# The last ranking of a four-layer expert kernel: row adds moved forward, final sums moved to another engine, 16-bit ranks, and matrix products that nobody reads

## The chip, the cores and the metric

The kernel runs on one core of a Trainium2 chip. A core has a matrix engine (PE, with its weight loads shown apart as PEld), a vector engine (DVE), a scalar or activation engine (ACT), a general engine (POOL, GpSimd) and SP, which here only issues transfers. Each engine takes its instructions in order; the engines run side by side and wait for one another on semaphores. Tiles live in on-chip memory with 128 partitions; PE writes its sums into PSUM.

The metric is the time of one execution on the device in microseconds (us). Before the change three runs took 1600.47, 1604.69 and 1605.46 us; the median is 1604.69.

## The reference

2048 tokens of 256 channels pass through four layers; each adds `ffn(cond(x))` to `x`. The change touches only the feed-forward part of the last layer, in which each of 16 experts takes at most 160 tokens, those with the highest gate value:

```python
cap = math.ceil(1.25 * bt / n)               # bt = 2048 tokens, n = 16 experts: 160
probs = softmax(x @ Wg)                      # (2048, 16)
top1_val, top1_idx = probs.max(-1), probs.argmax(-1)
masked = where(top1_idx[None, :] == arange(n)[:, None], top1_val[None, :], -inf)
vals, idx = top_k(masked, cap)               # per expert: its 160 best tokens
valid = isfinite(vals)
h = gelu(einsum('ncd,ndh->nch', x_flat[idx], W1) + b1[:, None, :])
out = einsum('nch,nhd->ncd', h, W2) + b2[:, None, :]
y_flat = x_flat.at[where(valid, idx, bt)].set(out, mode='drop')
# the layer before hands in x_flat; the kernel's result is x + y_flat
```

A token that no expert keeps passes `x_flat` itself on. So the result of every token is first `x + x_flat`, and the rows of the kept tokens are written again with `x + out`.

## The kernel before, in words

The 2048 tokens are 16 tiles of 128 (index t) and four blocks of 512 (index q). `Xt` holds the residual `x` by rows of tokens, `Ht` (in the memory `ACC`) the layer's input `x_flat` by rows, `HT` the same by channels.

**How `Ht` is finished.** The conditioning part of layer 3 (`_cond_moe`) ends with a shared expert, computed block by block in `_shared`: products `spg`, `spu`, a gate `sa` on DVE (L1232), products `spo` (L1235). Meanwhile the class `Tokens` adds the routed experts' rows: for each token tile SP loads two rows per token (`yt`), DVE adds them times a gate to `Ht` (L1321, two instructions a tile), and PE transposes the tile into `HT`. The list `by` says how many tiles have been added by each step of the last shared block; what is left is done by `pair`, two tiles a call, in `finish`.

**The last ranking** (class `Last`, four `chunk`s, one for each block q). A chunk is a list of small units:

- `logits`: writes the block to the DRAM tensor `hx` (its right half, written earlier, holds `Xt`), and multiplies it by the gate weights (`l3f_pt`).
- `top`: transposes the logits (`l3f_pl`); DVE finds the chosen expert and the softmax value.
- `rows`: DVE makes the one-hot of the expert (`l3f_oh`) and a bf16 row `l3f_z` of one-hot and the value split into three bf16 parts (with the small subtractions `l3f_r`, L1812); PE turns it (`l3f_ps`, L1816), and counts earlier tokens of the expert (`l3f_pn`).
- 4q+4 `beats`: one for each token tile t up to the block. A product `l3f_d` compares 128 tokens with 512; DVE (even t, L1855) or ACT (odd t, L1852) turns the signs into `l3f_b` and counts along the rows, and a second product adds them by columns (`l3f_cs`). After the last beat of a block `l3f_pc` brings the column counts into `l3f_acc`.

After `rows` of each block, `keep` adds `Ht` to `Xt` on GpSimd (L1876, 128x1024) and SP writes the block to the kernel's output (512 KB, L1877). Block 0's units and the first one of others are called by `plan` inside the steps of the shared expert; the rest in the order of the list `todo`, in `finish`, which a scheduler then spreads over the engines.

**From ranks to experts.** `l3f_acc` summed is twice each token's rank within its expert. DVE compares the rank with 0..159 (`l3f_A`, two halves of 128x1280, L1914), 32 products `l3f_pi` (L1919) turn that into the token of each rank, and DVE makes indices of them (`numbers`; `l3f_src`, and after a small product `l3f_pj` `l3f_srcg` for ranks 128 to 159 of four experts at a time). GpSimd gathers 128 rows of `hx` for each expert (L338) into one of six slots in `ACC`; PE transposes them (`ps_cm`, L360), multiplies (`l3f_ph`, `l3f_po`), and GpSimd scatters the result to the output. There are 16 such steps and four for the groups of four experts. The bias rows `b2` (for single experts) and `b2g` (for the groups) are loaded by SP, `b2g` into the memory of `Ht` once it is read.

Of the kernel before, what the change touches and what calls it, by code (L numbers as in the profile page):

```python
# [8 lines left out]
F32 = mybir.dt.float32  # L9
# [77 lines left out]
def _consts(k):  # L87
    nc, cp = k.nc, k.cp
    k.ident = cp.tile([P, P], F32, name="ident")
    make_identity(nc, k.ident)  # L90
    k.ones = cp.tile([P, P], F32, name="ones")
    nc.vector.memset(k.ones, 1.0)

    k.before = cp.tile([P, P], F32, name="before")
    nc.gpsimd.affine_select(out=k.before, in_=k.ones, compare_op=ALU.is_ge, fill=0.0,
                            base=-1, pattern=[[1, P]], channel_multiplier=-1)

    k.ident16 = cp.tile([P, P], BF16, name="ident16")
# [12 lines left out]
    nc.vector.tensor_copy(k.iota, ii)  # L111
    nc.vector.memset(k.zero[:, 0:D], 0.0)
    nc.vector.memset(k.zero[:, D:], NONE)
    it = cp.tile([P, NT], I32, name="it")
    nc.gpsimd.iota(it, pattern=[[P, NT]], base=0, channel_multiplier=1)
    k.tok = cp.tile([P, NT], F32, name="tok")
    nc.vector.tensor_copy(k.tok, it)
    k.tok2 = cp.tile([P, NT], F32, name="tok2")
    nc.vector.tensor_scalar_mul(k.tok2, k.tok, 2.0)
    k.one16 = cp.tile([P, P], BF16, name="one16")  # L120
    nc.vector.memset(k.one16, 1.0)
    k.two = cp.tile([P, 1], F32, name="two")
# [230 lines left out]
    return ps.rearrange("p c d -> p (c d)")  # L353


def _channel_major(k, psum, rows):

    ps = psum.tile([P, 2, P], F32, name="ps_cm", tag="t", bufs=2)
    for c in range(2):
        k.nc.tensor.transpose(ps[:, c, :], rows[:, c * P:(c + 1) * P], k.ident)  # L360
    return ps


# [845 lines left out]
                                             mybir.DependencyReason.SCHED_ONLY))  # L1209


def _shared(k, pool, psum, X, tb, W1, W3, W2, nf, hook=None, mid=None):


# [82 lines left out]
class Tokens:  # L1297
# [4 lines left out]
    def __init__(self, k, pool, psum, gate, dst, dstT, nf, next=None):  # L1302
        self.k, self.pool, self.psum, self.gate = k, pool, psum, gate
        self.dst, self.dstT, self.next = dst, dstT, next
        self.h = self.added = self.put = self.there = 0
        self.done = None
        self.mul = None

        self.by = [0, 0, 1, 3, 4, 6, 7, 9, 10, 12, 13, 15, 16, 16, 16, 16] if nf == 8 else \
                  [0, 0, 1, 3, 4, 6, 8, 10]  # L1310

    def add(self, t, ref=None):
        k, d = self.k, self.dst[:, t, :]
# [370 lines left out]
class Last:  # L1684
# [73 lines left out]
    def chunk(self, q):  # L1758
# [75 lines left out]
        def beats(t):  # L1834

            def unit(mul, mm):
# [27 lines left out]
                if t == 4 * q + 3:  # L1864
# [1 line left out]
                    nc.scalar.activation(less, got["cs"][0:1, :], AF.Copy, scale=-1.0)  # L1866
                    ps = psum.tile([P, 4], F32, name="l3f_pc", tag="t", bufs=2)
                    for j in range(4):
                        nc.tensor.matmul(ps[:, j:j + 1], less[:, j * P:(j + 1) * P], k.ones[0:1, 0:1],  # L1869
                                         start=True, stop=True, skip_group_check=True)  # L1870
                    nc.vector.tensor_copy(self.acc[:, ts, 6], ps)
            return unit

        def keep(mul, mm):
            x = k.Xt[:, ts, :]
            nc.gpsimd.tensor_tensor(x, x, k.Ht[:, ts, :], ALU.add)  # L1876
# [3 lines left out]
        def last(mul, mm):  # L1880
            rows(mul, mm)
            keep(mul, mm)

        return [logits, top, last] + [beats(t) for t in range(4 * q + 4)]

    def finish(self, c):

# [2 lines left out]
        for e in range(E):  # L1890
            nc.sync.dma_start(self.b2[:, e, :], k.A["L3_b2"][e:e + 1].to_broadcast([P, D]))
        self.weights()
        p0, p1, p2, p3 = self.parts
        todo = [c.pair, p0[0:2], p1[0:1], c.pair, p1[1:2], p0[2:4], c.pair, p2[0:1], p0[4:], p1[2:3], p2[1:2],
                p1[3:7], p3[0:1], p1[7:], p2[2:3], p3[1:2], p2[3:7], p3[2:3], p2[7:], p3[3:]]
        for x in todo:
            if callable(x):
                x()
            else:
                for p in x:  # L1900
                    p(None, None)
        assert c.put == NT
        self.b2g = k.Ht[:, 12:16, :]
# [4 lines left out]
        rank = k.rp.tile([P, NT], F32, name="l3f_rank")  # L1908
        nc.vector.tensor_reduce(rank, self.acc, AX.X, ALU.add)
        nc.vector.tensor_scalar_mul(rank, rank, 0.5)  # L1910
        ps = k.psum.tile([P, 2, 2, E], F32, name="l3f_pi", tag="t", bufs=2)
        for h in range(2):
            A = k.pool.tile([P, 8, CAP], BF16, name="l3f_A", tag="fa")
            nc.vector.tensor_tensor(A, _bc(k.iota, 1, [P, 8, CAP]),  # L1914
                                    _bc(rank[:, 8 * h:8 * h + 8], 2, [P, 8, CAP]), ALU.is_equal)
            for j in range(8):
                t = 8 * h + j
                for o, r in ((ps[:, 0], slice(0, P)), (ps[0:32, 1], slice(P, CAP))):
                    nc.tensor.matmul(o, A[:, j, r], self.ids[:, t], start=t == 0 and r.start == 0,  # L1919
                                     stop=t == NT - 1, skip_group_check=True)  # L1920
        self.src, self.dst = self.numbers(ps[:, 0], E, "")

        more = k.rp.tile([32, 2, E], F32, name="l3f_more")
        nc.vector.tensor_copy(more, ps[0:32, 1])
        pg = k.psum.tile([P, 2, 4], F32, name="l3f_pj", tag="t", bufs=2)
        for g in range(4):
            nc.tensor.matmul(pg[32 * g:32 * g + 32], k.ident[0:32, 0:32], more[:, :, g::4], start=True,
                             stop=True, skip_group_check=True)
        s, d = self.numbers(pg, 4, "g")
        self.src, self.dst = ([t[:, i:i + 1] for t, n in ((a, E), (b, 4)) for i in range(n)]  # L1930
                              for a, b in ((self.src, s), (self.dst, d)))

    def numbers(self, ps, n, name):

# [14 lines left out]
    def run(self):  # L1949
        k, nc, E, F = self.k, self.k.nc, self.E, self.F  # L1950
        pool, psum, b1 = k.pool, k.psum, k.small["L3_b1"]
        X = k.ACC.rearrange("p c s -> p (c s)").rearrange("p (b f) -> p b f", f=2 * D)

        order = [x for i in range(4) for x in (*range(4 * i, 4 * i + 4), E + i)]
        order = order[:-3] + [order[-1]] + order[-3:-1]
# [2 lines left out]
        def fetch(n):  # L1958
            if n < len(order):
                i = order[n]  # L1960
                at[i] = X[:, n % 6, :]
                _gather(k, at[i], k.hx, self.src[i])

        def end(i, po, b2):
# [54 lines left out]
            fetch(n)  # L2019
        for n, i in enumerate(order):  # L2020
            xT = pool.tile([P, 2, P], F32, name="xsT", bufs=3)
            nc.vector.tensor_copy(xT, _channel_major(k, psum, at[i]))
            if i < E:
                end(i, slot(i, xT), self.b2[:, i, :])
            else:
# [151 lines left out]
```

## Time and profile before

| what | value |
|---|---|
| median of three runs | 1604.69 us (1600.47 to 1605.46) |
| the profiled execution, and its span | 1597.45 us, 1595.3 us |
| mean granted clock of PE over the span | 0.964 |
| last shared block, to its last `spo` | until about 1434 us of the span |
| ranking: first `l3f_ps` | 1440.69 us |
| ranking: last copy of `l3f_pc` | 1483.99 us |
| one-hots `l3f_A` | 1484.80 us, 2.89 us for two |
| first gather issued, first transpose of gathered rows | 1492.58 us, 1496.12 us |
| experts at full clock | from about 1503.7 us |

The trace gives for each instruction its start and length, and what ended the idle time before it; `[2.70 <-DVE l3f_z L1810]` reads: the engine was idle for 2.70 us, until DVE's instruction of line 1810 was done. A group "x8" is eight instructions of one line in a row, with their busy time in sum. The windows give, for a stretch of the span, the busy time of each engine with its number of instructions, then the granted clock of PE (1.00 is full speed), the share of the transfer engines and GB/s. The chain of waits is the path back from the last instruction to what released each step.

### The profile page before, as it was taken

How to read it: one execution, taken by the hardware profiler on the slowest of the kernel's cores; microseconds unless marked ns; L12 is line 12 of the kernel's file. 1: busy time of each engine (PE TensorE's matmuls, PEld its weight loads, DVE VectorE, ACT ScalarE, POOL GpSimd, SP SyncE). 2: the span in 40 equal slices, each digit the busy share in tenths (PEclk: the TensorE clock that was granted, in tenths of full speed). 3: DMA queues.
4: the chain of work that ended last, by engine and by line, in shares of the span. 5: the costliest groups of instructions: out<-in, count | busy, mean ns of one | idle time of the engine just before them, and what ended most of it. 6: DMA issues, size and time to landing. Idle time of an engine off the chain costs nothing. (4 is left out here: it accounts for less than half of the span.)

```text
span 1595.3 us, 23657 instructions
## 1 busy us (share of the span) xinstructions
PE 1478.0 (93%) x8583; PEld 1024.6 (64%) x8586; DVE 475.0 (30%) x1586; ACT 303.3 (19%) x641; POOL 294.0 (18%) x321
## 2 busy tenths in 40 slices
PE   6979998967999989999999999999999999997797
PEld 2543333533555876555599999999995558864575
DVE  3732221323411344341111111111114414446332
ACT  2312221112111212111111111111112212125222
POOL 0400000200231332023100000000000163421242
PEclk9889999977999999999999999999999999998799
DMA  9769994813211465051152444255507357674171
GB/s 253 256 206 334 349 345 151 241 55 119 83 50 40 143 216 181 27 192 53 34 179 75 132 166 146 74 179 182 178 11 267 103 173 242 192 221 138 62 242 36
DMA packets 184242, 252.47 MB, mean 158 GB/s; under 512 B 17111, under 2 KB 137823, under 8 KB 184112
## 3 DMA queue, kind: packets, MB, share of 16 engines
q1 hardware_dynamic: 164448, 210.92, 40.7%
q0 software_dynamic: 14176, 36.63, 6.5%
q10 hardware_dynamic: 5488, 3.25, 0.7%
q8 instruction: 74, 1.21, 0.3%
q14 instruction: 56, 0.46, 0.1%
HBM read 284.86 MB, written 50.76 MB: 210 GB/s over the span
## 5 line engine op out<-in xcount | busy, mean ns | idle before, releaser
L283 POOL DMA_INDIRECT tbuf<-ys,sdst x114 | 112.2, 984 | 537.3 <-ACT ys L1438 228.4
L1235 PE MATMUL spo<-ring,sa 128*128 128x256 f32 x768 | 191.7, 392 | 14.0 <-DVE sa L1232 14.0
L1235 PEld LDWEIGHTS spo<-ring,sa 128*128 128x128 f32 x768 | 140.1, 191 | 95.9 <-DVE sa L1232 76.0
L1232 DVE TENSOR_TENSOR sa<-ssg,spu 128x512 f32<-128x512 f32 x96 | 65.9, 687 | 325.3 <-PE spu L1225 302.8
L1429 PE MATMUL fpg<-xsT,ring 128*128 128x128 f32 x1152 | 141.6, 276 | 5.9 <-ACT ys L1438 5.9
L1429 PEld LDWEIGHTS fpg<-xsT,ring 128*128 128x128 f32 x1152 | 135.8, 192 | 10.4 <-ACT ys L1438 9.4
L1429 PE MATMUL fpu<-xsT,ring 128*128 128x128 f32 x1152 | 140.4, 275 | 0.0
L1429 PEld LDWEIGHTS fpu<-xsT,ring 128*128 128x128 f32 x1152 | 134.4, 192 | 0.0
L1433 DVE TENSOR_TENSOR fa<-fsg,fpu 128x512 f32<-128x512 f32 x72 | 49.5, 688 | 276.9 <-PE fpu L1429 276.9
L1436 PE MATMUL fpo<-ring,fa 128*128 128x256 f32 x576 | 130.3, 379 | 0.0
L1230 ACT ACTIVATE ssg<-spg 128x512 f32<-128x512 f32 x96 | 57.3, 597 | 341.2 <-PE spg L1225 333.2
L1436 PEld LDWEIGHTS fpo<-ring,fa 128*128 128x128 f32 x576 | 106.7, 190 | 13.0
L1225 PE MATMUL spg<-HT,ring 128*128 128x512 f32 x192 | 101.2, 615 | 5.1 <-PEq L484 2.9
L1225 PE MATMUL spg<-XT,ring 128*128 128x512 f32 x192 | 99.0, 605 | 4.7 <-ACT XT L902 4.7
L1412 PE MATMUL cpo<-ring,ch 128*128 128x256 f32 x312 | 87.0, 402 | 5.8 <-ACT ch L1409 4.1
L1225 PE MATMUL spu<-HT,ring 128*128 128x512 f32 x192 | 91.1, 595 | 0.0
L1225 PE MATMUL spu<-XT,ring 128*128 128x512 f32 x192 | 90.5, 594 | 0.0
L1406 PEld LDWEIGHTS cph<-xsT,ring 128*128 128x128 f32 x624 | 81.8, 191 | 5.0 <-ACT ch L1409 1.1
L1406 PE MATMUL cph<-xsT,ring 128*128 128x128 f32 x624 | 82.4, 275 | 0.7 <-ACT ch L1409 0.7
L1379 DVE COPY xsT<-ps_cm 128x256 f32<-128x256 f32 x138 | 56.7, 422 | 82.5 <-PE ps_cm L360 81.9
L1432 ACT ACTIVATE fsg<-fpg 128x512 f32<-128x512 f32 x72 | 43.0, 597 | 179.6 <-PE fpg L1429 179.6
L1412 PEld LDWEIGHTS cpo<-ring,ch 128*128 128x128 f32 x312 | 53.1, 189 | 21.2 <-ACT ch L1409 15.1
(567 smaller groups left out, 1599.1 us busy)
## 6 DMA issues: line engine op xcount, KB each, us to landing
ring<-in_L_w SPq DMA_DIRECT2D x108, 1024.0 KB
ring<-in_L_r SPq DMA_DIRECT2D x96, 512.0 KB
ring<-in_L_r SPq DMA_DIRECT2D x156, 256.0 KB
xs<-xbuf SPq DMA_DIRECT2D x138, 129.0 KB
ring<-in_L_W SPq DMA_DIRECT2D x32, 512.0 KB
yt<-tbuf SPq DMA_DIRECT2D x48, 256.0 KB
xbuf<-ACC SPq DMA_DIRECT2D x1, 6063.0 KB
ring<-in_L_s SPq DMA_DIRECT2D x6, 512.0 KB
```

Of the source, the lines that this page charges most:

```text
L283: i = k.nc.gpsimd.indirect_dma_start(out=self.ap, out_offset=bass.IndirectOffsetOnAxis(ap=idx, axis=0), in_=rows, in_offset=None, **end)
L1225: mm = nc.tensor.matmul(ps, W[:, c, f * P:(f + 1) * P], X[:, c, cols], start=c == 0, stop=c == 1)
L1230: nc.scalar.activation(sg, pg, AF.Silu)
L1232: mul = nc.vector.tensor_mul(a, sg, pu)
L1235: mm = nc.tensor.matmul(po[g // 2][:, g % 2, :], a[:, g * P:(g + 1) * P], W2[:, f, :], start=f == 0 and g % 2 == 0, stop=f == nf - 1, skip ...
L1379: turned = nc.vector.tensor_copy(xT, _channel_major(k, self.psum, xs))
L1406: nc.tensor.matmul(ph[:, f, :], R1[:, c, f * P:(f + 1) * P], xT[:, c, :], start=c == 0, stop=c == 1)
L1412: nc.tensor.matmul(po, h[:, f, :], R2[:, f, :], start=f == 0, stop=f == 1)
L1429: nc.tensor.matmul(ps[:, j, :], W[:, c, (f0 + j) * P:(f0 + j + 1) * P], xT[:, c, :], start=c == 0, stop=c == 1)
L1432: nc.scalar.activation(sg, pg, AF.Silu)
L1433: nc.vector.tensor_mul(a[:, f0:f0 + 4, :], sg, pu)
L1436: nc.tensor.matmul(po, a[:, f, :], W2[:, f, :], start=f == 0, stop=f == 4 * nh - 1)
```

## The change

- `by` adds the row tiles earlier (12 instead of 10 within the shared steps), and `plan` has block 1's logits at the last of them.
- `todo` is reordered: both pairs of tiles first, then tops and rows of all blocks ahead of their beats; the 28 beats of blocks 2 and 3 come last, together.
- `keep` is gone. The four sums `Xt += Ht` are made by DVE behind the second `l3f_A`; the four writes of the output follow them, and the loads of `b2g` follow the writes.
- The ranks are compared in bf16, with a bf16 copy of the numbers 0..159.
- `_warm` adds six 128x512 bf16 products behind the last `l3f_pc`, ahead of `l3f_pi`, and ten behind `l3f_pj`, ahead of the first `ps_cm`. Nothing reads their results.
- The gathers go to `HT`, which has eight slots, instead of `ACC` with six.

As the scheduler places it, DVE's order at the end is: both `l3f_A`, the sum of block 0, the copy of `l3f_pi`, the sum of block 1, four more small steps, the sum of block 2, the cast `l3f_src`, three steps and the cast `l3f_dst`, the sum of block 3, the rest. Line numbers in the kernel after are those of before plus 2 from L112 on and plus 4 to 17 in the functions below.

```diff
+    k.iota16 = cp.tile([P, CAP], BF16, name="iota16")
+    nc.vector.tensor_copy(k.iota16, ii)
...
+def _warm(k, psum, ref, n):
+    ps = psum.tile([P, TB], F32, name="warm", tag="mm")
+    for _ in range(n):
+        i = k.nc.tensor.matmul(ps.rearrange("p (j q) -> p j q", q=P), k.ident16, _bc(k.ident16, 1, [P, 4, P]),
+                               start=True, stop=True, skip_group_check=True)
+        _behind(k, i, ref)
+        ref = i
+    return ref
...
-                  [0, 0, 1, 3, 4, 6, 8, 10]
+                  [0, 0, 2, 4, 6, 8, 10, 12]
...
-        self.plan = {5: [0], 6: [0], 7: [0]}
+        self.plan = {5: [0], 6: [0], 7: [0, 1]}
...
-        def keep(mul, mm):
-            x = k.Xt[:, ts, :]
-            nc.gpsimd.tensor_tensor(x, x, k.Ht[:, ts, :], ALU.add)
-            i = nc.sync.dma_start(k.out[cols, :].rearrange("(t p) d -> p t d", p=P), x)
-            self.outs.append(i.ins.name)
...
-        todo = [c.pair, p0[0:2], p1[0:1], c.pair, p1[1:2], p0[2:4], c.pair, p2[0:1], p0[4:], p1[2:3], p2[1:2],
-                p1[3:7], p3[0:1], p1[7:], p2[2:3], p3[1:2], p2[3:7], p3[2:3], p2[7:], p3[3:]]
+        todo = [c.pair, c.pair, p1[0:1], p2[0:1], p3[0:1], p0, p2[1:2], p1[1:2], p3[1:2], p1[2:], p2[2:3],
+                p3[2:3], p2[3:], p3[3:]]
...
+        ref = _warm(k, k.psum, ref, 6)
...
+        rank16 = k.rp.tile([P, NT], BF16, name="l3f_rank16")
+        nc.vector.tensor_scalar_mul(rank16, rank, 0.5)
...
-            nc.vector.tensor_tensor(A, _bc(k.iota, 1, [P, 8, CAP]),
-                                    _bc(rank[:, 8 * h:8 * h + 8], 2, [P, 8, CAP]), ALU.is_equal)
+            made = nc.vector.tensor_tensor(A, _bc(k.iota16, 1, [P, 8, CAP]),
+                                           _bc(rank16[:, 8 * h:8 * h + 8], 2, [P, 8, CAP]), ALU.is_equal)
...
+        self.ref = _warm(k, k.psum, ref, 10)
...
+        for q in range(NB):
+            x = k.Xt[:, 4 * q:4 * q + 4, :]
+            _behind(k, nc.vector.tensor_tensor(x, x, k.Ht[:, 4 * q:4 * q + 4, :], ALU.add), made)
+            i = nc.sync.dma_start(k.out[q * TB:(q + 1) * TB, :].rearrange("(t p) d -> p t d", p=P), x)
+            self.outs.append(i.ins.name)
         self.b2g = k.Ht[:, 12:16, :]
...
-        X = k.ACC.rearrange("p c s -> p (c s)").rearrange("p (b f) -> p b f", f=2 * D)
+        X = k.HT.rearrange("p c n -> p (c n)").rearrange("p (b f) -> p b f", f=2 * D)
...
-                at[i] = X[:, n % 6, :]
+                at[i] = X[:, (n + 4) % 8, :]
```

`_behind` orders one instruction after another on its engine. `_channel_major` makes `ps_cm`, and its transposes now stand behind the ten products.

More of the change, by code (lines that the diff above doesn't have):

```diff
@@ L353, in _token_major, with _channel_major @@
     return ps.rearrange("p c d -> p (c d)")
-def _channel_major(k, psum, rows):
+def _channel_major(k, psum, rows, ref=None):
     ps = psum.tile([P, 2, P], F32, name="ps_cm", tag="t", bufs=2)
     for c in range(2):
-        k.nc.tensor.transpose(ps[:, c, :], rows[:, c * P:(c + 1) * P], k.ident)
+        i = k.nc.tensor.transpose(ps[:, c, :], rows[:, c * P:(c + 1) * P], k.ident)
+        if ref is not None:
+            _behind(k, i, ref)
     return ps
@@ L1209, in _behind @@
                                              mybir.DependencyReason.SCHED_ONLY))
+def _warm(k, psum, ref, n):
[3 more added lines that the diff above has]
+                               start=True, stop=True, skip_group_check=True)
+        _behind(k, i, ref)
+        ref = i
+    return ref
 def _shared(k, pool, psum, X, tb, W1, W3, W2, nf, hook=None, mid=None):
@@ L1868, in unit @@
                     for j in range(4):
-                        nc.tensor.matmul(ps[:, j:j + 1], less[:, j * P:(j + 1) * P], k.ones[0:1, 0:1],
+                        i = nc.tensor.matmul(ps[:, j:j + 1], less[:, j * P:(j + 1) * P], k.ones[0:1, 0:1],
                                          start=True, stop=True, skip_group_check=True)
                     nc.vector.tensor_copy(self.acc[:, ts, 6], ps)
+                    return i
             return unit
-        def keep(mul, mm):
-            x = k.Xt[:, ts, :]
-            nc.gpsimd.tensor_tensor(x, x, k.Ht[:, ts, :], ALU.add)
-            i = nc.sync.dma_start(k.out[cols, :].rearrange("(t p) d -> p t d", p=P), x)
-            self.outs.append(i.ins.name)
[L1880 to L1884, printed above, removed]
+        return [logits, top, rows] + [beats(t) for t in range(4 * q + 4)]
     def finish(self, c):
@@ L1893, in finish @@
         p0, p1, p2, p3 = self.parts
-        todo = [c.pair, p0[0:2], p1[0:1], c.pair, p1[1:2], p0[2:4], c.pair, p2[0:1], p0[4:], p1[2:3], p2[1:2],
-                p1[3:7], p3[0:1], p1[7:], p2[2:3], p3[1:2], p2[3:7], p3[2:3], p2[7:], p3[3:]]
+        todo = [c.pair, c.pair, p1[0:1], p2[0:1], p3[0:1], p0, p2[1:2], p1[1:2], p3[1:2], p1[2:], p2[2:3],
+                p3[2:3], p2[3:], p3[3:]]
+        ref = None
         for x in todo:
@@ L1900, in finish @@
                 for p in x:
-                    p(None, None)
+                    ref = p(None, None) or ref
+        ref = _warm(k, k.psum, ref, 6)
         assert c.put == NT
+        rank = k.rp.tile([P, NT], F32, name="l3f_rank")
+        nc.vector.tensor_reduce(rank, self.acc, AX.X, ALU.add)
+        rank16 = k.rp.tile([P, NT], BF16, name="l3f_rank16")
+        nc.vector.tensor_scalar_mul(rank16, rank, 0.5)
+        ps = k.psum.tile([P, 2, 2, E], F32, name="l3f_pi", tag="t", bufs=2)
+        for h in range(2):
+            A = k.pool.tile([P, 8, CAP], BF16, name="l3f_A", tag="fa")
+            made = nc.vector.tensor_tensor(A, _bc(k.iota16, 1, [P, 8, CAP]),
+                                           _bc(rank16[:, 8 * h:8 * h + 8], 2, [P, 8, CAP]), ALU.is_equal)
+            for j in range(8):
+                t = 8 * h + j
+                for o, r in ((ps[:, 0], slice(0, P)), (ps[0:32, 1], slice(P, CAP))):
+                    i = nc.tensor.matmul(o, A[:, j, r], self.ids[:, t], start=t == 0 and r.start == 0,
+                                         stop=t == NT - 1, skip_group_check=True)
+                    _behind(k, i, ref)
+        self.src, self.dst = self.numbers(ps[:, 0], E, "")
+        more = k.rp.tile([32, 2, E], F32, name="l3f_more")
+        nc.vector.tensor_copy(more, ps[0:32, 1])
+        pg = k.psum.tile([P, 2, 4], F32, name="l3f_pj", tag="t", bufs=2)
+        for g in range(4):
+            ref = nc.tensor.matmul(pg[32 * g:32 * g + 32], k.ident[0:32, 0:32], more[:, :, g::4], start=True,
+                                   stop=True, skip_group_check=True)
+        self.ref = _warm(k, k.psum, ref, 10)
+        s, d = self.numbers(pg, 4, "g")
+        self.src, self.dst = ([t[:, i:i + 1] for t, n in ((a, E), (b, 4)) for i in range(n)]
+                              for a, b in ((self.src, s), (self.dst, d)))
+        for q in range(NB):
[3 more added lines that the diff above has]
+            self.outs.append(i.ins.name)
         self.b2g = k.Ht[:, 12:16, :]
@@ L1907, in finish @@
                               k.A["L3_b2"][e:e + 1].to_broadcast([32, D]))
[L1908 to L1914, printed above, removed]
-                                    _bc(rank[:, 8 * h:8 * h + 8], 2, [P, 8, CAP]), ALU.is_equal)
[L1916 to L1931, printed above, removed]
     def numbers(self, ps, n, name):
@@ L2021, in run @@
             xT = pool.tile([P, 2, P], F32, name="xsT", bufs=3)
-            nc.vector.tensor_copy(xT, _channel_major(k, psum, at[i]))
+            nc.vector.tensor_copy(xT, _channel_major(k, psum, at[i], self.ref))
             if i < E:
```

## The prediction

> **What bounds the kernel now.** I read the page first, for the whole, then the windows of the stage that changes (1422 to 1505 us of the span), then its timeline on each engine, and last the chain of waits. The page:
>
> ```profile
> span 1595.3 us, 23657 instructions
> ...
> PE 1478.0 (93%) x8583; PEld 1024.6 (64%) x8586; DVE 475.0 (30%) x1586; ACT 303.3 (19%) x641; POOL 294.0 (18%) x321
> ...
> PEclk9889999977999999999999999999999999998799
> ```
>
> TensorE is the bound of the span, but the share says nothing of 83 us in the last tenth, where the granted clock dips (digits 8, 7). The windows there (columns: PE, PEld, DVE, ACT, POOL, granted clock, DMA share):
>
> ```profile
> 1440.00:1452.00 12.00, 9.41 (x76) 5.98 (x76) 7.13 (x31) 4.91 (x15) 0.54 (x1) 0.73 0.66 236
> 1452.00:1462.00 10.00, 6.79 (x46) 3.97 (x47) 7.13 (x33) 3.97 (x11) 1.96 (x1) 0.64 0.43 144
> ...
> 1472.00:1484.00 12.00, 10.88 (x62) 5.78 (x61) 6.21 (x22) 8.63 (x23) 0.00 (x0) 1.00 0.01 2
> 1484.00:1492.00 8.00, 4.82 (x40) 3.51 (x40) 4.46 (x14) 0.15 (x1) 0.00 (x0) 0.65 0.00 0
> ...
> 1496.00:1500.00 4.00, 3.19 (x14) 2.85 (x15) 0.42 (x1) 0.00 (x0) 2.93 (x4) 0.50 0.66 205
> ```
>
> PE has holes in 1440–1462 and, after its last beat, in 1484–1500; in both the clock falls to about half. Finer windows put the half-clock stretches at 1442.5–1445.5, 1449–1459.1 and 1486.5–1503.7. The timeline says who makes the holes:
>
> ```profile
> 1451.46 2.49 POOL L1876 TENSOR_TENSOR Xt<-Xt,ACC 128x1024 f32<-128x1024 f32 x1 [13.12 <-DVE ACC L1321]
> ...
> 1451.64 2.33 DVE L1812 TENSOR_TENSOR l3f_r<-l3f_val,l3f_z 128x4 f32<-128x4 f32 x1
> ...
> 1454.80 1.03 PE L1816 MATMUL l3f_ps<-ident,l3f_z 128*128 128x128 bf16 x8 [2.70 <-DVE l3f_z L1810]
> ...
> 1462.59 0.61 PE L1816 MATMUL l3f_ps<-ident,l3f_z 128*128 128x128 bf16 x8
> ...
> 1468.76 0.62 PE L1816 MATMUL l3f_ps<-ident,l3f_z 128*128 128x128 bf16 x8 [0.72 <-DVE l3f_z L1810]
> ...
> 1483.99 0.17 DVE L1871 COPY l3f_acc<-l3f_pc 128x4 f32<-128x4 f32 x1 [2.51 <-PE l3f_pc L1869]
> ...
> 1484.80 2.89 DVE L1914 TENSOR_TENSOR l3f_A<-iota,l3f_rank 128x1280 bf16<-128x1280 f32 x2
> ...
> 1486.35 4.53 PE L1919 MATMUL l3f_pi<-l3f_ids,l3f_A 128*128 128x32 bf16 x32 [2.40 <-DVE l3f_A L1914]
> ...
> 1491.54 0.17 DVE L1942 CAST l3f_src<-l3f_i 128x16 uint32<-128x16 f32 x1
> ...
> 1492.58 1.00 POOL L338 DMA_INDIRECT ACC<-hx,l3f_src  x1 [38.63 <-DVE l3f_i2g L1943]
> ...
> 1496.12 0.66 PE L360 MATMUL ps_cm<-ident,ACC 128*128 128x128 f32 x2 [4.30 <-DMA ACC<-hx,l3f_src]
> ```
>
> A four-column subtraction that takes 0.16 us elsewhere takes 2.33 us beside GpSimd's add, and PE's rows of block 1 (`ps` at 1454.80) wait for it. From 1484 on nothing overlaps: rank, one-hots, `pi`, indices, gather, first expert. The chain of waits runs the same way:
>
> ```profile
> 1451.72 2.25 DVE l3f_r L1812
> ...
> 1454.80 1.03 PE l3f_ps L1816 x8
> ...
> 1486.35 4.54 PE l3f_pi L1919 x32
> ...
> 1493.89 3.45 DMA ACC<-hx,l3f_src
> ...
> 1497.92 3.41 PE l3f_ph L1980 x16
> ```
>
> **The change, part by part** (us; before is always the profiled execution).
>
> *Row adds earlier, logits of block 1 at step 7.* Two pairs of token rows instead of three remain after the last shared step. Steps there wait on row loads: DVE waited 4.29, 0.36 and 2.75 on `yt` (1418.07, 1420.43, 1431.24), and PE's `spo` waited 0.91, 0.41 and 0.95 on DVE's `sa` behind them. One more add now stands before the second `sa`, whose rows land about 1419.4 by the issue pitch of 0.85; that `spo` comes 1.1 to 1.5 later, and the later two waits shrink, because SP no longer issues the first `out` write (1425.16) ahead of their loads. Net +0.9 at the last `spo`, bounds 0 and +1.5. The rows of block 3 still load behind `b2` and a weight on SP (1430.63 to 1436.26): 0 to +2, inside the bounds below. The writes of `hx`, of blocks 2 and 3, move ahead of `out`; the last was issued 41 before the first gather: 0, and it would cost only if that cover shrank below the 3.45 a gather takes.
>
> *Final sums off GpSimd.* Its four adds (2.36, 2.35, 2.35, 2.49) go. Two held DVE up: 2.42 at 1436.01 where 0.22 is usual, and 2.33 at 1451.64. The first gives back 2.2, which covers the late start: `ps` of block 0 comes at 1440.3 instead of 1440.7. The second, and logits made earlier, bring `ps` of block 1 from 1454.80 to 1450.3 (bounds 1449.3, all of 5.4 gained, and 1451.3).
>
> *The new order.* Block 1 to block 2: eight beats at 0.527 (the last 24 beats took 12.6, 1469.66 to 1482.3) = 4.2, `pn` 0.85, `pc` 1.05, the transpose and its pause 0.9: 7.0, so 1457.3. Block 2 to the end of block 3's `pn` took 7.27 with four beats between; without them 7.27 - 2.1 = 5.2, and 0.6 less where the `z` wait of 0.72 runs beside `pn`: 4.6, so 1461.9. Then 28 beats, 14.75, to 1476.65; from the last beat to the copy of `pc` 1.7 (1482.3 to 1483.99): 1478.4. That is **-5.6** against 1483.99. The bounds: 0, if the beats in one run wait for `b` slots and PE's clock as much as the mixed order did; -9, if none of PE's holes stays (they sum to 10.8 in 1435–1484, less what rows must still wait). I take -5.6, nearest to the rows of 1469–1484, which are already such a run of beats and at full clock.
>
> *Ranks compared in bfloat16.* The two one-hots took 2.89, 1.45 each. Bounds: 0, and half of it, -0.75 for the first and -1.45 in all. I take 0. The trace has no 16-bit compare of a broadcast operand; casts of `z` to bf16 show nothing faster than their f32 neighbours (0.23 beside 0.22). [...] The extra copy of iota at the start is one 128x160 copy, under 0.3 in a DVE idle for 70%: 0, or +0.3 without that cover.
>
> *Products nobody reads, before `pi`.* Six 512-column bf16 products, 0.215 each at full clock, 1.3 in all, stand in PE's wait of 2.40 for the first one-hot. Alone they cost 0 (+1.3 if the wait were gone). If PE keeps the full clock, `pi` and `pj` end about 1.9 sooner after the second one-hot (32 products that spread over 1487.7–1490.9 at half clock). Bounds 0 and -1.9.
>
> *Sums on DVE behind the one-hots.* Four adds of 128x1024. Rows: 128x512 f32 at 0.687, 128x1280 at 1.45; between them 1.14 each. DVE is in order, and two of them end up inside the chain of indices (after the first index steps and ahead of the cast of `src`): +2.3 (one, +1.1; none, if they fit the wait of 3.22 for `pi`, 0). With the gain of `pi`, copy of `pc` to cast of `src` is 7.74 instead of 7.55: **+0.2**, +2.1 if the clock falls first.
>
> *Writes of `out` late.* Four writes of 512 KB, on SP, no longer beside the ranking but beside the first gathers; the 16 loads of `b2g` queue behind them (first used at the fifth gather's expert group, far later). At the 380 to 390 GB/s seen in 1441–1446 a write takes 1.4. The first gather took 3.45; behind one or two writes it takes +0.5 to +2.8. I take **+1.0**, since two of the four sums come after the index cast. Scatters wait for these writes too, but start some 15 later. Gathers into HT (eight slots for six) let GpSimd issue eight ahead of the first scatter instead of six: one each 1.25, nobody waits for the sixth: 0 to -0.3.
>
> *Products before the first transpose.* Ten, 2.2 at full clock; PE waits 4.30 for the gather. If they held the clock, `ph` and `po` would not start at half rate to 1503.7: -3.0 (six of half-clock stretch, 1497.7–1503.7). The trace's clock edges at 1442.45, 1445.5, 1448.96, 1459.1, 1486.5 and 1503.7 lie on one grid of about 3.41. [...] By the grid of the trace alone the bounds are the same, 0 and -3.0; I take half, **-1.6**.
>
> Sum: -5.6 + 0.2 + 1.0 - 1.6 = **-6.0**. The experts from 1505 to 1586 are PE at clock 1.00 with the same products, and the last scatters follow them: unchanged. On the profiled execution, 1597.45 - 6.0 = 1591.4 (its span 1595.3 and 2.15 around it). That execution lies 7.2 below the median of the three runs, 1604.69, so the median becomes 1598.7; I give **1598**, a shade lower, as more of the bounds lie below -6.0 than above.
>
> **The rivals.** (a) *Slower: the clock stays low in the ranking.* At half clock a bf16 product takes 0.43 (`cs`, 1458.60) and a beat has two: 0.86 instead of 0.527. If the tops and rows of blocks 1 to 3, now gathered at 1441–1462, leave PE short of work long enough that the clock is still half during the 36 beats behind them, they cost 36 x 0.333 = +12; less 5.6, and with the tail's +0.2 + 1.0 and no clock gain there: +7.6, 1612. From 28 beats at half clock on it passes +4.8. For it: windows of 0.73 and 0.64 at a PE duty of 0.68 to 0.78. Against: 28 beats in one run are at 0.91 duty and 1.00. (b) *The tail takes it back:* three sums in the index chain (+3.4), two writes ahead of the gather (+2.8), no clock gained: +5 to +6, against -5.6: 0 for the whole, about 1604. For it: DVE in order, and a DMA queue that was empty (0.01, 0.00) and no longer is. Against: the first sums fit PE's time in `pi`. (c) *More:* -9 in the ranking, clock kept to the experts (-3), the gather undisturbed: -11 to -12, 1593. (d) *The parts do nothing:* beats stay bound at 0.527 with the old holes moved, 16-bit compare and products without effect: -1 to -2, 1603.
>
> **How the numbers follow.** Chances: forecast (-4 to -9) 0.50, (c) 0.17, (b) 0.11, (d) 0.09, (a) 0.13. What a measurement can tell from no change is 0.3%, 4.8. Faster by more: 0.46 of the forecast, all of (c), 0.04 of (b) and (d) in milder forms: 0.67. Same: 0.04 of the forecast, 0.12 of (b) and (d), 0.02 of a mild (a): 0.18. Slower: 0.11 of (a), and 0.04 for (b) with nothing gained in the ranking: 0.15. The range reaches from (c) counted from the lowest run, 1600.47 - 11 = 1589.5, to (b) at the highest, 1605.46, so 1606; it leaves out (a) and a few of (c). For the forecast alone, 1595.7 to 1600.7.
>
> **What would show it.** Right: no 2.3 stall on `r` and no POOL add; `ps` of block 1 near 1450; the copy of `pc` near 1478; the one-hots still 1.45 each; two sums of about 1.1 to 1.2 between the index steps; the first gather's landing 3.5 to 5 after issue; the experts' clock back within 3 of `ps_cm`. Wrong: granted clock under 0.8 in windows of the last beats; beats slower than 0.55; DVE still in a sum when PE has finished `pj` for 2 us; a first `ps_cm` that waits over 6. I would be most wrong if the clock in the ranking, which I read from windows, is set by something other than PE's own holes.

## The result and the profile after

The kernel after took 1603.66 us (median of 20 runs, 1598.26 to 1608.57), the kernel before 1603.61 us (20 runs). The ratio is 0.9996, 95% interval 0.9984 to 1.0009: no difference that can be told. (The ratio is that of the means of the 20 runs; the medians are as good as equal.) The forecast of 1598 us is missed by 5.7 us. The time lies in the range, which holds no change at all as well, at the place where rival (b) had put it; the prediction gave "faster" 0.67 and "same" 0.18.

The profiled execution of after took 1608.57 us, with a span of 1606.7 us, 11 us longer than the one of before. Those 11 us lie ahead of the changed stage: the first `spo` of the last shared block starts at 1425.32 us instead of 1414.36 (in the experiments below, between 1411.82 and 1423.55). So the two traces are compared by stages counted from that `spo`, in us:

| stage | before | after | difference | forecast |
|---|---|---|---|---|
| first `spo` to last copy of `l3f_pc` | 69.63 | 66.07 | -3.56 | -5.6 |
| copy of `l3f_pc` to cast of `l3f_src` | 7.55 | 9.13 | +1.58 | +0.2 |
| cast of `l3f_src` to first `ps_cm` | 4.58 | 7.02 | +2.44 | +1.0 |
| first `ps_cm` to the end | 99.18 | 99.16 | 0.0 | -1.6 |
| sum | 180.94 | 181.38 | +0.4 | -6.0 |

The first `spo`, before and after:

```profile
1414.36 1.89 PE L1235 MATMUL spo<-ring,sa 128*128 128x256 f32 x8
...
1425.32 1.89 PE L1250 MATMUL spo<-ring,sa 128*128 128x256 f32 x8
```

The ranking gave two thirds of what was forecast, and the tail took it all back. The page of after:

```profile
span 1606.7 us, 23696 instructions
...
PE 1484.9 (92%) x8602; PEld 1028.1 (64%) x8602; DVE 474.1 (30%) x1591; ACT 303.8 (19%) x641; POOL 285.0 (18%) x317
...
PEclk9889999977999999999999999999999999998899
```

POOL has lost 9 us, its four sums; DVE, which now makes them (4.9 us), has gained none: its two long stalls, 4.4 us above the usual length, are gone. Where the gain of the ranking went does not show on the page. It shows in the timeline of after, from the second `spo` of the stage on:

```profile
1431.65 3.24 PE L1250 MATMUL spo<-ring,sa 128*128 128x256 f32 x8 [1.86 <-DVE sa L1247]
...
1463.92 0.62 PE L1831 MATMUL l3f_ps<-ident,l3f_z 128*128 128x128 bf16 x8 [1.12 <-DVE l3f_z L1825]
...
1491.39 0.17 DVE L1886 COPY l3f_acc<-l3f_pc 128x4 f32<-128x4 f32 x1 [2.51 <-PE l3f_pc L1884]
...
1492.21 2.89 DVE L1918 TENSOR_TENSOR l3f_A<-iota,l3f_rank 128x1280 bf16<-128x1280 bf16 x2
1493.75 4.01 PE L1923 MATMUL l3f_pi<-l3f_ids,l3f_A 128*128 128x32 bf16 x32 [0.99 <-DVE l3f_A L1918]
...
1496.26 6.24 SPq L1942 DMA_DIRECT2D out<-Xt  x4
1497.80 0.17 DVE L1954 COPY l3f_i<-l3f_pi 128x16 f32<-128x16 f32 x1 [1.57 <-PE l3f_pi L1923]
1497.89 1.22 DVE L1941 TENSOR_TENSOR Xt<-Xt,ACC 128x1024 f32<-128x1024 f32 x1
...
1499.39 1.22 DVE L1941 TENSOR_TENSOR Xt<-Xt,ACC 128x1024 f32<-128x1024 f32 x1
...
1500.52 0.17 DVE L1959 CAST l3f_src<-l3f_i 128x16 uint32<-128x16 f32 x1
...
1501.55 1.41 POOL L340 DMA_INDIRECT HT<-hx,l3f_src  x1 [78.63 <-DVE l3f_i0g L1954]
...
1507.54 0.66 PE L362 MATMUL ps_cm<-ident,HT 128*128 128x128 f32 x2 [3.46 <-DMA HT<-hx,l3f_src]
```

The tail in two steps: between the copy of `l3f_pi` and the cast of `l3f_src` stand two sums of 1.22 us (0.63 us from copy to cast before, 2.72 now), and the first gather, issued at 1501.55 us after three writes of the output, feeds `ps_cm` 5.99 us later instead of 3.54. The copy of before, whose cast is at 1491.54:

```profile
1490.91 0.17 DVE L1937 COPY l3f_i<-l3f_pi 128x16 f32<-128x16 f32 x1 [3.22 <-PE l3f_pi L1919]
```

The one-hots take 2.89 us for two, as before, with all operands in bf16. The chain of waits of after names the same steps:

```profile
1497.98 1.13 DVE Xt L1941
1499.48 1.13 DVE Xt L1941
...
1501.55 5.85 DMA HT<-hx,l3f_src
1507.54 0.66 PE ps_cm L362 x2
```

The windows of after, cut at the changes of the clock (columns PE, PEld, DVE, ACT, POOL, granted clock, DMA share, GB/s):

```profile
1494.00:1497.40 3.40, 3.40 (x29) 2.64 (x28) 2.23 (x2) 0.00 (x0) 0.00 (x0) 0.95 0.06 20
1497.40:1500.50 3.10, 1.44 (x14) 0.73 (x14) 2.70 (x7) 0.00 (x0) 0.00 (x0) 0.50 0.57 195
1500.50:1504.00 3.50, 3.50 (x9) 1.03 (x7) 2.38 (x12) 0.00 (x0) 2.15 (x2) 0.51 1.00 337
1504.00:1507.50 3.50, 0.07 (x1) 0.00 (x0) 0.00 (x0) 0.00 (x0) 2.59 (x4) 0.98 0.95 287
1507.50:1514.50 7.00, 6.33 (x27) 5.40 (x28) 1.18 (x3) 1.14 (x4) 3.33 (x4) 0.52 0.79 266
```

The clock falls near 1497.1 (a mean of 0.95 in the first row), while `l3f_pi` still runs, to 1497.76. The ten products, at half rate 4.43 us long, keep PE busy for all of the third row, and the clock is back at 1503.9. But PE then has nothing until 1507.5 (0.07 of 3.50 us in the fourth row), and the experts start at half rate after all (0.52 in the last).

Rows of 1 us show the writes in the last two columns:

```profile
1498.00:1499.00 1.00, 0.00 (x0) 0.00 (x0) 1.00 (x1) 0.00 (x0) 0.00 (x0) 0.50 0.73 247
1499.00:1500.00 1.00, 0.57 (x9) 0.35 (x10) 1.00 (x6) 0.00 (x0) 0.00 (x0) 0.50 0.00 0
1500.00:1501.00 1.00, 1.00 (x4) 0.40 (x3) 1.00 (x6) 0.00 (x0) 0.00 (x0) 0.50 0.92 322
...
1504.00:1505.00 1.00, 0.07 (x1) 0.00 (x0) 0.00 (x0) 0.00 (x0) 0.69 (x2) 1.00 1.09 270
```

By the transfer records of the trace the first write is through at 1498.8, the other three move from 1500.0 to 1505.0, and the first rows of the gather move at 1504.93, 3.38 us after its issue; before, 1.69 us after.

### The profile page after: what moved, and what is told of

It reads as the page before. It is cut to its first block, busy times and chain, and to the rows that moved or that the text cites. A ratio compares the mean times of both kernels' runs of the same rounds, so it can differ in the third digit from the quotient of the medians.

```text
span 1606.7 us, 23696 instructions
## 1 busy us (share of the span) xinstructions
PE 1484.9 (92%) x8602; PEld 1028.1 (64%) x8602; DVE 474.1 (30%) x1591; ACT 303.8 (19%) x641; POOL 285.0 (18%) x317
```

## The experiments

Totals below are ratios to the kernel before, run beside each kernel on the same chip; the kernel before itself took 1597.9 to 1606.3 us there (medians), so bare times of different experiments are not compared. A stage length is from one profiled execution.

**1. Without the unread products.**

```diff
-        ref = _warm(k, k.psum, ref, 6)
...
-        self.ref = _warm(k, k.psum, ref, 10)
+        self.ref = ref
```

> The kernel after without the 6 and the 10 products that nobody reads; all else as after. Theory A (the products do next to nothing, because the clock falls in the gather wait all the same): the copy of l3f_pc to the cast of l3f_src stays within 0.6 us of after's 9.13, the first ps_cm to the fifth step's ps_cm is as long as in after, the total is within 1 us of after. Theory B (the products hold the clock as I forecast): l3f_pi takes 1.9 us longer and the experts start at half clock for up to 3 us more, the total is 3 to 5 us longer than after.

Measured: ratio 0.9994 (0.9977 to 1.0010). The copy of `l3f_pc` to the cast took 9.66 us (after: 9.13), the cast to the first `ps_cm` 6.53 (7.02), from there to the end 99.44 (99.16). Theory A: the products are worth 0.5 us in `l3f_pi`, and nothing that shows in the total.

**2. Without the writes of the output.**

```diff
-            i = nc.sync.dma_start(k.out[q * TB:(q + 1) * TB, :].rearrange("(t p) d -> p t d", p=P), x)
-            self.outs.append(i.ins.name)
```

> The kernel after without the four writes of the output that follow the sums (so tokens that no expert keeps are not written; the sums are still made). Theory A (the first gather queues behind the writes): the first gather lands in 3.4 to 3.8 us instead of 5.85, the first ps_cm comes 2.0 to 2.4 us sooner after the cast of l3f_src. Rival (the gather is slow for another reason: GpSimd's descriptors, 1.41 us instead of 1.00, held up by DVE's sum, or the new slots in HT): the first gather still takes over 5 us.

Measured: ratio 0.9983 (0.9967 to 1.0000), not to be told from after. The timeline of this kernel, which leaves the rows that no expert keeps unwritten:

```profile
1497.77 0.17 DVE L1957 CAST l3f_src<-l3f_i 128x16 uint32<-128x16 f32 x1
...
1498.80 1.41 POOL L340 DMA_INDIRECT HT<-hx,l3f_src  x1 [78.53 <-DVE l3f_i0g L1952]
1499.43 7.33 SPq L1945 DMA_DIRECT2D ACC<-in_L_b  x16
...
1503.44 0.41 PE L362 MATMUL ps_cm<-ident,HT 128*128 128x128 f32 x2 [2.10 <-DMA HT<-hx,l3f_src]
```

The cast to the first `ps_cm` takes 5.67 us: 1.35 of the 2.44 us go with the writes. The other 1.1 stay, between the two expectations. GpSimd's part of the gather is still 1.41 us long where 1.00 is usual, and the 16 loads of `b2g`, no longer held back by the writes, now run beside the gather. The transfer records divide the 1.1 us: the first rows move 2.12 us after the issue (1.69 before), 0.4 more, and from there to `ps_cm` it takes 2.52 us (1.85 before), 0.7 more. The first part goes with GpSimd's longer one, the second falls beside the loads; that the loads cause it was not tested.

**3. The sums behind the last index step.**

```diff
-            _behind(k, nc.vector.tensor_tensor(x, x, k.Ht[:, 4 * q:4 * q + 4, :], ALU.add), made)
+            _behind(k, nc.vector.tensor_tensor(x, x, k.Ht[:, 4 * q:4 * q + 4, :], ALU.add), self.last)
...
-        nc.vector.tensor_copy(dst, t[2])
+        self.last = nc.vector.tensor_copy(dst, t[2])
```

> The kernel after with the four sums on DVE behind the last cast of indices (l3f_dstg) instead of between the index steps. Theory A: the copy of l3f_pc to the cast of l3f_src falls from 9.13 us by two sums of 1.13 to 6.9, the first write is issued behind the first gather, which lands in 3.5 to 4.2 us; the first ps_cm comes 3.5 to 4.5 us sooner after the copy of l3f_pc than in after, and the total is 3 to 4 us below before. Rival (the time only moves on: the sums now hold up the copies xsT of the first experts, and the writes the gathers behind them): the first ps_cm comes sooner but the fifth step's ps_cm stands where it stood in after.

Measured: ratio 0.9951 (0.9930 to 0.9972), 7.8 us by the ratio, where 3 to 4 were expected. The copy of `l3f_pc` to the cast took 7.02 us, the cast to the first `ps_cm` 4.48, from there to the end 97.96; the sum of stages is 174.96, 6.0 below before. The rival is seen too, but costs less than the gain:

```profile
1487.60 4.63 DVE L1941 TENSOR_TENSOR Xt<-Xt,ACC 128x1024 f32<-128x1024 f32 x4
...
1489.96 1.95 POOL L340 DMA_INDIRECT HT<-hx,l3f_src  x1 [0.30 <-DVE Xt L1941]
1490.74 0.66 PE L362 MATMUL ps_cm<-ident,HT 128*128 128x128 f32 x2
...
1493.49 0.41 PE L362 MATMUL ps_cm<-ident,HT 128*128 128x128 f32 x2 [2.09 <-DMA HT<-hx,l3f_src]
```

The second gather's rows come 2.75 us after the first's (1.35 before). What this experiment shows is where the gain of after went: only the place of the four sums, and of the writes that follow them, differs from after, and the intervals of the two ratios lie apart. What share the sums have in it and what share the writes, it does not tell.

**4. The three orders alone, in the kernel before.**

```diff
-                  [0, 0, 1, 3, 4, 6, 8, 10]
+                  [0, 0, 2, 4, 6, 8, 10, 12]
...
-        self.plan = {5: [0], 6: [0], 7: [0]}
+        self.plan = {5: [0], 6: [0], 7: [0, 1]}
...
-        todo = [c.pair, p0[0:2], p1[0:1], c.pair, p1[1:2], p0[2:4], c.pair, p2[0:1], p0[4:], p1[2:3], p2[1:2],
-                p1[3:7], p3[0:1], p1[7:], p2[2:3], p3[1:2], p2[3:7], p3[2:3], p2[7:], p3[3:]]
+        todo = [c.pair, c.pair, p1[0:1], p2[0:1], p3[0:1], p0, p2[1:2], p1[1:2], p3[1:2], p1[2:], p2[2:3],
+                p3[2:3], p2[3:], p3[3:]]
```

> The kernel before with only the three orders of the kernel after (row adds per step, plan, list of units); sums on GpSimd, f32 ranks, no products, gathers into ACC. If the ranking's 3.6 us (first spo of the last shared block to the last l3f_pc: 68.55 before, 64.99 after) come from the order: 64 to 66 us, and with before's tail (13.2 us from the last l3f_pc to the first ps_cm) the total is 2.5 to 4 us below before. Rival (they come from GpSimd's adds going, each of which stalls DVE for over 2 us): 67 to 70 us, no gain.

Measured: ratio 0.9990 (0.9974 to 1.0005); first `spo` to copy of `l3f_pc` 69.84 us. The rival, to the letter: with GpSimd's sums in place the new order gains nothing that can be told. They stall DVE as before, only at other instructions (2.58 us for a row add that takes 0.48 beside it, 1.54 us for a one-hot of 0.21 to 0.23):

```profile
1441.18 2.72 POOL L1876 TENSOR_TENSOR Xt<-Xt,ACC 128x1024 f32<-128x1024 f32 x1 [5.50 <-DVE l3f_f L1795]
...
1441.60 2.58 DVE L1321 SCALAR_TENSOR_TENSOR ACC<-yt,l3c_g,ACC 128x256 f32<-128x256 f32 x1
...
1453.01 2.35 POOL L1876 TENSOR_TENSOR Xt<-Xt,ACC 128x1024 f32<-128x1024 f32 x1 [9.11 <-DVE l3f_val L1797]
...
1453.90 1.54 DVE L1802 TENSOR_TENSOR l3f_oh<-l3f_down,l3f_f 128x64 f32<-128x64 f32 x1
```

**5. The sums last, one tile of row adds fewer at the third step.**

```diff
-                  [0, 0, 2, 4, 6, 8, 10, 12]
+                  [0, 0, 1, 4, 6, 8, 10, 12]
```

> The kernel with the sums last, and only one tile of rows instead of two added at the third step (by = 0, 0, 1, 4, 6, 8, 10, 12). If the two row adds that stand ahead of the second sa cost what they seem to (PE's second spo waits 1.8 to 2.0 us in the kernels with two, 0.91 before, and in some executions an idle clock window then makes it 3.2 to 3.7 us long): the second spo waits 0.9 us, first spo to copy of l3f_pc falls from 65.5 to 64 or less, the total is 1 to 2 us under the kernel with the sums last. Rival: the wait is made up later, because the ranking waits on the last row loads anyway; 65 to 66 us, no difference.

Measured: ratio 0.9955 (0.9940 to 0.9970), not to be told from experiment 3. In the trace the second `spo` waits 0.70 us and runs at full clock, and the ranking takes 62.75 us instead of 65.50; the stages sum to 173.47.

```profile
1425.99 1.99 PE L1250 MATMUL spo<-ring,sa 128*128 128x256 f32 x8 [0.70 <-DVE sa L1247]
```

The shorter wait is shown, its worth is not: the totals don't resolve it, and experiments 9 and 10, with one tile fewer as well, took 65.33 and 64.86 us in the ranking.

**6. The sums last, the old orders.** The three edits of experiment 4 undone in the kernel of experiment 3.

> The kernel with the sums last, and the three orders (by, plan, list of units) of the kernel before. First spo to copy of l3f_pc: 69.63 before, 69.84 with the new order and GpSimd's sums, 65.5 to 66.3 with the new order and no sums there. Theory A (the adds on GpSimd were the whole cost, the order is worth nothing by itself): 65.5 to 66.5. Theory B (the two need one another: the order helps once DVE isn't held up): 67.5 to 69, the total 2 to 3 us over the kernel with the sums last.

Measured: ratio 0.9980 (0.9966 to 0.9994); first `spo` to copy of `l3f_pc` 66.33 us:

```profile
1416.64 1.89 PE L1250 MATMUL spo<-ring,sa 128*128 128x256 f32 x8
...
1453.14 1.04 PE L1831 MATMUL l3f_ps<-ident,l3f_z 128*128 128x128 bf16 x8 [0.72 <-DVE l3f_z L1825]
...
1482.97 0.17 DVE L1886 COPY l3f_acc<-l3f_pc 128x4 f32<-128x4 f32 x1 [2.51 <-PE l3f_pc L1884]
```

With experiment 4 this makes the square: old order and GpSimd's sums 69.63, new order with them 69.84, old order without 66.33, new order without 64.33 to 66.27 (experiments 1, 2, 3, 7 and after, whose ranking is the same code, so that their spread of 1.9 us is that of single traces). The step of 3.3 us or more comes with the sums leaving GpSimd, whichever the order. The order is worth 0.1 to 2.0 us in this stage, no more than that spread; the total here is 4.6 us above that of experiment 3 by the central values (0.9980 and 0.9951), whose intervals overlap, and the trace puts 2.4 of it behind the first `ps_cm` (100.37 and 97.96).

**7. The sums last, without the unread products.** The edits of experiment 1 in the kernel of experiment 3.

> The kernel with the sums last, without the products that nobody reads. In after they were worth about 0.1 us up to the first ps_cm. With the sums last PE's gap before the first ps_cm is 4.5 us and ten products at half clock fill it, and the clock was back at 1.00 at 1492, ahead of the first l3f_ph. Theory A (this is their worth): first ps_cm to the end grows from 97.96 to 99 to 100.5, copy of l3f_pc to cast of l3f_src from 7.02 to 7.5; total 1.5 to 3 us over the kernel with the sums last. Theory B (they do nothing here either): within 0.5 us in both.

Measured: ratio 0.9969 (0.9950 to 0.9988). The copy of `l3f_pc` to the cast took 7.57 us (7.02 with products), the first `ps_cm` to the end 100.03 (97.96). The stages fit theory A; the totals, 0.9969 and 0.9951, overlap.

**8. The sums on DVE among the last 28 beats.** `self.beat` is DVE's last comparison of a beat; a sum stands behind it, and its write follows at once.

```diff
+        def keep(q):
+            def unit(mul, mm):
+                x = k.Xt[:, 4 * q:4 * q + 4, :]
+                _behind(k, nc.vector.tensor_tensor(x, x, k.Ht[:, 4 * q:4 * q + 4, :], ALU.add), self.beat)
+                i = nc.sync.dma_start(k.out[q * TB:(q + 1) * TB, :].rearrange("(t p) d -> p t d", p=P), x)
+                self.outs.append(i.ins.name)
+            return [unit]
...
-                p3[2:3], p2[3:], p3[3:]]
+                p3[2:3], p2[3:8], keep(0), p2[8:13], keep(1), p2[13:], p3[3:6], keep(2), p3[6:11], keep(3), p3[11:]]
```

> The kernel after with the four sums on DVE and their writes spread among the last 28 beats instead of behind the one-hots. Theory A (DVE has room there, 6.9 of 12 us busy, and the queue is empty, DMA share 0.01): first spo to copy of l3f_pc 66 to 67 instead of 66.07, the cast of l3f_src 7.0 after the copy of l3f_pc, the first gather 3.5 us, the second ps_cm not late as with the sums last (2.75 after the first); total 1 us under to 1 us over the kernel with the sums last. Rival (the beats feed PE closely, so each sum of 1.13 us holds PE up): 69 to 70.5 us, and the gain over before is lost.

Measured: ratio 0.9971 (0.9937 to 1.0005). In the trace it is the shortest of all by stages, 172.89: ranking 64.12, copy to cast 7.08, cast to first `ps_cm` 4.59, from there 97.10. The groups of the last beats, 1460 to 1476 us:

```profile
L1878 PE MATMUL l3f_cs<-l3f_b,one 128*128 128x512 bf16 (+3 forms) x28 | 9.0, 373 | 1.4 <-DVE l3f_b L1870 0.9 <-issue 0.2 <-ACT l3f_b L1867 0.2
...
L1904 DVE TENSOR_TENSOR Xt<-Xt,ACC 128x1024 f32<-128x1024 f32 x4 | 4.9, 1222 | 0.0
```

Four sums of 1.22 us cost PE 0.9 us of waiting for DVE (in the same beats of experiment 3 PE never waited for DVE); in front of the gathers two of them had cost 2.1. The ratio, with its wide interval, does not tell this kernel from before or from experiment 3.

**9. Both findings: the sums among the beats, and one tile fewer.** The edits of 5 and 8 together.

> Both findings together: the sums on DVE among the last 28 beats, and one tile of row adds at the third step. If they add: first spo to copy of l3f_pc 61 to 62.5 (64.12 less the 1.6 to 2.7 that the one tile was worth), copy of l3f_pc to first ps_cm 11.7, first spo to the end 170 to 171.5 against 180.94 before, and the total 8 to 10 us below before (ratio 0.994 to 0.995). Rival (the start's gain is swallowed by the beats, which then wait for DVE's sums): first spo to the end 172.5 to 173.5, as with either alone.

Measured: ratio 0.9936 (0.9915 to 0.9956), 10.3 us below before and the lowest ratio of this study, though the intervals of experiments 3, 5, 7, 8 and 10 overlap with it. The stages don't follow: 65.33 us in the ranking where 61 to 62.5 were expected, 175.75 in sum. The traces differ in the clock. The half-rate time of the ranking was 6.8 us in experiment 8, 7.0 in 5, 10.2 in 2, 3 and 7, 13.7 in before and after, 14.0 here and 17.1 in 4: close to whole numbers of 3.4 us, from two to five, in kernels that differ little. With the spread of 1.9 us under experiment 6, one profiled execution tells a stage only to about 1 to 2 us, and the ratio is the better evidence for the sum.

**10. The same, without the unread products.**

> The same without the products that nobody reads. Sums last, they were worth 0.53 in copy of l3f_pc to first ps_cm and 2.07 from there to the end (100.03 against 97.96). If that holds with an undisturbed first gather: copy of l3f_pc to first ps_cm 12.1 to 12.3, first ps_cm to the end 99 to 100 against 97.1, total 2 to 3 us over the kernel with them. Rival (the difference was that of two executions): within 1 us.

Measured: ratio 0.9959 (0.9944 to 0.9974), over 11 executions; a twelfth took 3802.95 us and is left out. The copy of `l3f_pc` to the first `ps_cm` took 12.13 us (11.71 with them), from there to the end 98.43 (98.71). The first six products save 0.4 to 0.6 us here as in 1 and 7; the ten before `ps_cm` gained 2.1 us in one pair of traces and nothing in the other two. The totals, 0.9936 and 0.9959, overlap.

**11. One word changed in the kernel before.**

```diff
-            nc.gpsimd.tensor_tensor(x, x, k.Ht[:, ts, :], ALU.add)
+            nc.vector.tensor_tensor(x, x, k.Ht[:, ts, :], ALU.add)
```

> The kernel before with one word changed: the four sums on DVE instead of GpSimd, at the same places; orders, f32 ranks, slots as before, no products. Each of the two sums that hold up the rows of a block then costs DVE 1.13 us instead of 2.2 to 2.3. If the shared stall was the cost: first spo to copy of l3f_pc 67 to 68.5 (69.63 before, 66.33 without sums there), the tail as before (12.1), total 1 to 2.5 us below before. Rival (GpSimd's stall is as long as the sum on DVE plus what the sums in the shared steps now cost): 69 to 70, no gain.

Measured: ratio 0.9974 (0.9959 to 0.9989), 4.2 us (1.8 to 6.6) where 1 to 2.5 were expected; first `spo` to copy of `l3f_pc` 67.10 us, the tail 12.08. As expected, a sum in the rows of block 1 now costs DVE its own length and no more:

```profile
1457.05 1.22 DVE L1876 TENSOR_TENSOR Xt<-Xt,ACC 128x1024 f32<-128x1024 f32 x1
1458.19 0.16 DVE L1812 TENSOR_TENSOR l3f_r<-l3f_r,l3f_z 128x4 f32<-128x4 f32 x1
```

## Why the prediction was right and wrong

- **Row adds earlier (+0.9 forecast, bounds 0 and +1.5):** +1.9, outside the bounds: the first `spo` to the end of the last one took 23.34 us after 21.44. The second `spo` came 0.96 us later, near the 1.1 to 1.5 of the forecast, behind a wait of 1.86 us. What was left out is the clock: at 1432.24 it fell, after 3.41 us in which PE was busy for 1.55, and the eight products took 3.24 us where they take 1.99 at full clock. At this `spo` the clock fell behind waits of 1.86 to 2.02 us (after, experiments 1, 3 and 4) and stayed at 1.00 behind waits of 1.78 to 1.81 (2, 7 and 8), in single traces. Where it stays (experiments 2 and 7: 21.6) the cost is 0.1 to 0.2.
- **Sums off GpSimd and the new order (-5.6):** -3.56. Of the 5.6 the prediction put 4.5 on `l3f_ps` of block 1 coming sooner (bounds 3.5 and 5.5), and this step failed: counted from the first `spo`, it came 1.85 us sooner (38.59 after 40.44). That GpSimd's sums had cost so much holds, for without them in the old order it came at 36.50, 3.9 sooner (experiment 6). What the sum took as covered is the late start: `l3f_ps` of block 0 came 0.8 us later (27.17 after 26.34) where 0.4 sooner was forecast, and in experiments 2 and 7, where the second `spo` ran at full clock, it came at 25.43. From `l3f_ps` of block 1 to the copy 1.7 us were gained where 1.1 was forecast, although the last 28 beats with their end took 17.25 us from `l3f_pn` to the copy, not 16.45, 2.5 us of it at half clock. All these are from single traces.
- **bf16 ranks (0):** right; 2.89 us both times, from f32 operands in before and bf16 in after. The casts of `z`, 0.23 beside 0.22, pointed that way; why 16 bits bring nothing here, no run shows.
- **Products before `l3f_pi` (0 to -1.9, taken at -1.9):** 0.4 to 0.6 us, by experiments 1, 7 and 10. This term failed because it took `l3f_pi` to go with the clock: at full clock for 3.3 us of its length it still took 4.01 us for 4.53, about 0.12 us for each product at full clock and 0.13 to 0.14 at half (before).
- **Sums behind the one-hots (+2.3 for two in the chain):** right to 0.2: +2.1 from the copy of `l3f_pi` to the cast. The stage as a whole missed (+1.58 for +0.2) because the products' gain was to pay for it. (The two terms as written, +2.3 and -1.9, make +0.4, not the +0.2 of the forecast.)
- **Writes of `out` (+1.0, bounds +0.5 and +2.8):** +2.44, inside the bounds. The reason given for the low value, that two sums come after the cast, didn't hold: three stand ahead of it, as the order listed under "The change" already has it, and the gather's rows moved only when the last three writes were through (at 1504.93 and 1505.0 us). By experiment 2 1.35 us belong to the writes.
- **Products before the first transpose (-1.6):** 0. Half of the 3.0 was the author's estimate, and no run shows it: with and without the unread products the first `ps_cm` to the end took 97.96 and 100.03 us in one pair of traces (experiments 3 and 7), 99.16 and 99.44 (after and 1) and 98.71 and 98.43 (9 and 10) in the others. In after the longer gather left PE a gap of 3.46 us behind the products, and the clock fell at 1507.33, so the two last terms were not independent, though they were added as if they were. A gather of the usual length was no safeguard: in experiments 9 and 10 (4.58 and 4.56 us from the cast to `ps_cm`) the ten products were worth nothing either.
- **The rivals:** (b) came, with two sums in the chain instead of three. That its number, 1604, fits so well is partly luck: the ranking gained 3.6 us instead of its 5.6, and the tail lost 4.0 instead of its 5 to 6. It had 0.11 of the chances; its parts were all in the sum already, most of them taken on their hopeful side. Rival (d), also near in number (1603), is not what happened, since the stages moved by up to 3.6 us. Rival (a), a clock that stays low in the ranking, did not come; the half-rate time there was 13.7 us in both traces.

## What to carry to other kernels

Work that is moved off a busy stage has to land somewhere with slack in all that it brings: here four sums and 2 MB of writes went from a stage with GpSimd's stalls to the one stretch where nothing overlaps, and the same edit with the sums and writes a few instructions later was 0.5% faster. Among the beats before it was 0.3%, not clear of noise, and 0.6% with one tile fewer. When a sum of terms holds several that share one wait (here the gather), they are to be costed together, at the end where they meet.

The half-rate time of the ranking differed by up to three stretches of 3.4 us between nearly equal kernels, and the same ranking code took 64.33 to 66.27 us in five traces, so a gain of 2 us in one trace needs a second trace or a ratio over many runs.

## What the runs showed that was not expected

- The half-rate stretches were whole multiples of 3.41 us: from the stage's first `spo` to 1510 us they were 3.41, 10.24 and 17.07 us long in before, and to 1515 us 3.41, 6.83, 3.41, 6.83 and 6.83 us in after.
- The clock fell to half although PE was busy by the records: in after from 1493.75 us on, all of it in `l3f_pi` (32 products of 32 columns), and half rate came near 1497.1, while they still ran. In the kernel with the sums last it fell near 1485.1, inside the same products, which ran from 1481.60 to 1485.59. In the 3.41 us ahead of the fall PE was busy for 3.34 us in after and for 3.41 in experiments 2, 3 and 9; in before, it was busy for only 1.96 of the 3.41 us from 1465.99 on, and the clock stayed full. So the records' busy share alone does not tell when the clock falls; what it goes by, no run shows.
- GpSimd's part of a gather, 0.94 to 1.00 us for the first six in before and in experiments 4, 8 and 11, took 1.41 us in after and experiments 1 and 2 and up to 1.95 us in experiment 3 while DVE made sums, and never over 0.98 us for the first gathers in experiment 8, where the sums were long done. Another gather beside a sum took 1.07 us, so the sum alone isn't shown to be the cause.
- A sum on DVE of 1.22 us costs less than the same sum on GpSimd, which takes 2.35 to 2.49 us in before and holds DVE up for most of it (2.33 us for a subtraction of 0.16), where the kernel waits for DVE: one word, 4.2 us (1.8 to 6.6).
